# Value product of an attention layer turned round: v stationary on two column halves of the array, queries moving, probabilities divided on GpSimd

## The chip, the cores and the metric

One core of one Trainium2 chip. The metric is the device time of one launch in microseconds, median of several runs. In the profile PE is TensorE (PEld its weight loads), DVE is VectorE, ACT is ScalarE, POOL is GpSimd.

## The reference, cut to what matters

Input x has 64 batches of 256 tokens with 512 features, float32. Layer 0 is a graph attention, layer 1 a masked attention of 8 heads of 64 columns. Each is `x + layer(relu(layernorm(x)))`.

```
# layer 1, h = relu(layernorm(x)); adj is one 256x256 mask for all batches
q, k, v = split_heads(h @ Wq.T + bq), split_heads(h @ Wk.T + bk), split_heads(h @ Wv.T + bv)
scores = einsum('bhqd,bhkd->bhqk', q, k) / sqrt(64)
attn = softmax(where(adj == 0, -inf, scores))
out = einsum('bhqk,bhkd->bhqd', attn, v)         # <- the value product
return merge_heads(out) @ Wo.T + bo
```

## The kernel before

It works in 32 groups of two batches, that is four tiles of 128 tokens. Layer 0 of the next group is issued among layer 1 of this one. A unit of layer-1 attention is one tile and four heads, and unit n's values are issued behind unit n+1's scores:

```python
def values(t, hq, pr):                       # pr: numerators, queries on the partitions
    ...
    for i in range(2):
        # transpose two heads: keys onto the partitions
        nc.tensor.transpose(pp[:, r, kc, :], pr[:, 2 * i + r, kc * P : (kc + 1) * P], ident)
        ...copy pp to pT, DVE for i = 0, ACT for i = 1...
        nc.tensor.matmul(
            pav[:, h * DH : (h + 1) * DH],                  # [128 queries, 64]
            pT[:, r, kc, :],                                # stationary: 128x128 probabilities
            v[:, b * NC + kc, h * DH : (h + 1) * DH],       # moving: 64 columns
            start=(kc == 0), stop=(kc == NC - 1))

def finish(t):                               # once per tile
    nc.vector.reciprocal(rc, sm)
    nc.vector.tensor_mul(av, pav, rc)                       # normalise the output (broadcast cut)
    ...four transposes of av into pa, ACT copy to aT, output projection, residual, store...

for t in range(NT):
    for hq in range(2):
        pr = scores(t, hq)
        yield
        if pending is not None:
            values(*pending)
            if pending[1] == 1:
                finish(pending[0])
            yield
        pending = (t, hq, pr)
```

Layer 0 runs on the same engines in the same stretch:

```python
nc.vector.tensor_reduce(nmx, z, AX.X, ALU.max)                                  # 128x2
nc.vector.tensor_scalar(nmx, nmx, FLOOR, -1.0, op0=ALU.max, op1=ALU.mult)       # "the negation"
...exponentials on ACT, transposes pp, copy pT, then the layer-0 product po...
```

## Time and profile before

| | before |
|---|---|
| time, us (median; range) | 3982.18 (3979.65 to 3984.23) |
| mean granted clock | 0.998 |
| one group, us | 123.2: projections 55.1, attention 68.1 |

The page, the chain of waits and the timeline of one group are shown in the prediction. One more view of the kernel before cuts the attention stretch of that group (1963.60 to 2031.70) into pieces. The columns are start:end, length, then busy us of PE, PEld, DVE, ACT and POOL (with their instructions), the granted clock (PEclk), the DMA share and GB/s:

```profile
core 0: us, PE busy (x) PEld busy (x) DVE busy (x) ACT busy (x) POOL busy (x), PEclk, DMA share, GB/s
1963.60:1978.60 15.00, 14.56 (x86) 9.98 (x86) 13.99 (x55) 9.04 (x32) 0.00 (x0) 1.00 0.01 2
1978.60:1993.60 15.00, 14.82 (x68) 8.74 (x68) 9.28 (x27) 4.04 (x14) 0.00 (x0) 1.00 0.05 17
1993.60:2008.60 15.00, 14.79 (x91) 10.20 (x90) 12.05 (x40) 6.28 (x20) 4.57 (x4) 1.00 0.05 19
2008.60:2031.70 23.10, 20.84 (x127) 14.85 (x125) 9.06 (x21) 10.31 (x29) 2.88 (x2) 1.00 0.09 28
```

(The page counts records: the 2048 value matmuls of the program stand there as 4096, two each.) DVE, with 13.99 of 15 us, is the busiest engine of the opening after PE itself (14.56). One row of that group's timeline is for later: the first transposes of numerators, 4.57 us into the stretch.

```profile
1968.17 1.91 PE L322 MATMUL pp<-ident,pr 128*128 128x128 f32 x8
```

### The profile page before, as it was taken

Reading aid. Unit: us, or ns where it says so; the run is one execution under the profiler, and the core shown is the slowest. Engines: PE = TensorE matmul, PEld = TensorE weight load, DVE = VectorE, ACT = ScalarE, POOL = GpSimd, SP = SyncE. Lnnn points to the kernel's source line nnn. Section 1 sums busy time; section 2 is a strip of 40 time slices with the busy share of each in tenths; the row PEclk is TensorE's granted clock in tenths of the full one; section 3 lists DMA queues with packets and bytes.
Section 4 is the critical chain, followed back from the end, with each engine's and each line's share of the span. In section 5 each row is a group of like instructions: output and inputs, shape, how many; then the busy total and the mean of one; then the engine's idle time right before and its main releaser. Section 6 shows DMA issues by size and latency. Waiting matters only on the chain.

```text
span 3978.6 us, 41676 instructions
## 1 busy us (share of the span) xinstructions
PE 3853.1 (97%) x15744; PEld 2182.8 (55%) x15744; DVE 1732.9 (44%) x5186; ACT 1109.1 (28%) x3201; POOL 247.8 (6%) x206
## 2 busy tenths in 40 slices
PE   7999999999999999999999999999999999999999
PEld 3555555555555555555555555555555555555555
DVE  3444344443345433454334543344443444433442
ACT  1322223222233222332223322233222232222332
POOL 1000000000000000000000000000000000000000
PEclk9999999999999999999999999999999999999999
DMA  2000000000000000000000000000000000000000
GB/s 98 22 9 16 19 22 22 9 16 19 22 22 14 13 17 22 22 22 6 19 19 22 22 6 19 19 22 22 9 16 19 22 22 9 16 19 22 11 11 11
DMA packets 39144, 76.33 MB, mean 19 GB/s; under 512 B 3297, under 2 KB 3297, under 8 KB 38945
## 3 DMA queue, kind: packets, MB, share of 16 engines
q1 hardware_dynamic: 38480, 72.36, 5.0%
q8 instruction: 124, 2.03, 0.2%
q0 software_dynamic: 464, 1.32, 0.1%
q14 instruction: 76, 0.61, 0.1%
HBM read 40.11 MB, written 33.55 MB: 19 GB/s over the span
## 4 chain that ended last, share of the span: by engine, by line
PE 87%; DVE 9%; ACT 3%; issue 1%; DMA 0%; POOL 0%; POOLq 0%; DVEq 0%; ACTq 0%
PE pav L333 12%; PE po L150 12%; PE pq L157 11%; PE pw L150 11%; PE pv L150 11%; PE pk L157 11%; PE psc L281 5%; PE pp L322 5%; PE po L223 4%; ACT hT L143 2%; PE pa L354 2%; DVE s L292 2%; PE pt L142 2%; DVE av L346 2%; DVE x L230 1%; DVE junk L174 1%
## 5 line engine op out<-in xcount | busy, mean ns | idle before, releaser
L333 PEld LDWEIGHTS pav<-v,pT 128*128 128x128 f32 x4096 | 498.8, 191 | 136.5 <-issue 45.9
L308 ACT ACTIVATE pr<-s,nmx 128x256 f32<-128x256 f32 x1024 | 507.0, 497 | 180.1 <-DVE nmx L304 157.9
L333 PE MATMUL pav<-v,pT 128*128 128x64 f32 x4096 | 525.0, 276 | 6.9 <-DVE pT L329 4.8
L150 PE MATMUL po<-wo_sb,aT 128*128 128x512 f32 x1024 | 474.2, 606 | 3.2 <-ACT aT L356 0.7
L157 PE MATMUL pq<-hT,wq_sb 128*128 128x512 f32 x1024 | 463.6, 595 | 7.9 <-ACT hT L143 7.9
L157 PE MATMUL pk<-hT,wk_sb 128*128 128x512 f32 x1024 | 460.3, 592 | 0.0
L150 PE MATMUL pw<-w_sb,hT 128*128 128x512 f32 x1024 | 460.1, 592 | 0.0
L150 PE MATMUL pv<-wv_sb,hT 128*128 128x512 f32 x1024 | 444.7, 592 | 0.0
L252 DVE TENSOR_SCALAR kT<-pk,bk_c 128x512 f32<-128x512 f32 x128 | 96.1, 751 | 776.0 <-PE pk L157 776.0
L281 PE MATMUL psc<-kT,qT 64*128 64x256 f32 x2048 | 399.0, 413 | 8.4 <-DVE mx L292 6.4
L292 DVE CUSTOM_DVE_ANT_0 s<-psc,mbias 128x256 f32<-128x256 f32 x1024 | 384.3, 417 | 11.1 <-PE psc L281 6.8
L171 ACT COPY wh<-pw 128x512 f32<-128x512 f32 x128 | 74.9, 585 | 1100.2 <-PE pw L150 1100.2
L157 PEld LDWEIGHTS pk<-hT,wk_sb 128*128 128x128 f32 x1024 | 194.6, 190 | 244.9 <-issue 244.9
L150 PEld LDWEIGHTS pv<-wv_sb,hT 128*128 128x128 f32 x1024 | 194.6, 190 | 244.9 <-issue 244.9
L150 PEld LDWEIGHTS pw<-w_sb,hT 128*128 128x128 f32 x1024 | 194.7, 190 | 244.5 <-issue 244.5
L157 PEld LDWEIGHTS pq<-hT,wq_sb 128*128 128x128 f32 x1024 | 191.9, 190 | 245.2 <-issue 229.6
L322 PE MATMUL pp<-ident,pr 128*128 128x128 f32 x2048 | 311.6, 277 | 5.0
L327 ACT COPY pT<-pp 128x512 f32<-128x512 f32 x256 | 149.1, 582 | 581.1 <-PE pp L322 578.2
L150 PEld LDWEIGHTS po<-wo_sb,aT 128*128 128x128 f32 x1024 | 184.4, 190 | 217.3 <-issue 184.1
L322 PEld LDWEIGHTS pp<-ident,pr 128*128 128x128 f32 x2048 | 234.3, 145 | 83.6 <-issue 44.1
L281 PEld LDWEIGHTS psc<-kT,qT 64*128 64x128 f32 x2048 | 220.9, 185 | 100.1 <-issue 56.8
L174 DVE SCALAR_TENSOR_TENSOR junk<-wh,a_dst_b 128x512 f32<-128x512 f32 x128 | 88.5, 691 | 421.4 <-ACT wh L171 421.4
(57 smaller groups left out, 3103.3 us busy)
## 6 DMA issues: line engine op xcount, KB each, us to landing
x<-in_x_dram SPq DMA_DIRECT2D x64, 512.0 KB, 4.4
out_dram<-x SPq DMA_DIRECT2D x128, 256.0 KB, 2.0
w_sb<-in_L_gnn_W_dram SPq DMA_DIRECT2D x1, 1024.0 KB, 13.3
wq_sb<-in_L_gnn_Wq_dram SPq DMA_DIRECT2D x1, 1024.0 KB, 15.9
wk_sb<-in_L_gnn_Wk_dram SPq DMA_DIRECT2D x1, 1024.0 KB, 18.1
wv_sb<-in_L_gnn_Wv_dram SPq DMA_DIRECT2D x1, 1024.0 KB, 20.1
wo_sb<-in_L_gnn_Wo_dram SPq DMA_DIRECT2D x1, 1024.0 KB, 16.1
a_src_b<-in_L_gnn_a_src_dram POOLq DMA_DIRECT2D x1, 256.0 KB, 6.8
```

Source lines behind the costliest of these rows:

```text
L142: nc.tensor.transpose(pt[:, c, :], xn[:, c * P : (c + 1) * P], ident)
L150: nc.tensor.matmul(dst, hT[:, c, t * P : (t + 1) * P], w_t[:, c, :], start=(c == 0), stop=(c == DC - 1))
L157: nc.tensor.matmul(dst, w_t[:, c, e * P : (e + 1) * P], hT[:, c, :], start=(c == 0), stop=(c == DC - 1))
L174: nc.vector.scalar_tensor_tensor(junk, wh[:, t, :], 1.0, a, op0=ALU.mult, op1=ALU.mult, accum_out=dst[:, t : t + 1])
L223: nc.tensor.matmul(po, pT[:, mc, c * P : (c + 1) * P], wh[:, b * NC + mc, :], start=(mc == 0), stop=(mc == NC - 1),)
L252: nc.vector.tensor_scalar_add(kT[:, e, :], pk, bk_c[:, e : e + 1])
L281: nc.tensor.matmul(psc[r][:, i, :], qT[rows, e, t * P : (t + 1) * P], kT[rows, e, b * N : (b + 1) * N], start=True, stop=True,)
L292: nc.vector.tensor_tensor_reduce(out=s[:, j, :], in0=psc[r][:, i, :], in1=mbias[:, c, :], scale=1.0, scalar=FLOOR, op0=ALU.add, op1=ALU.ma ...
L308: nc.scalar.activation(pr[:, j, :], s[:, j, :], AF.Exp, bias=nmx[:, j : j + 1], accum_out=sm[:, h : h + 1])
L322: nc.tensor.transpose(pp[:, r, kc, :], pr[:, 2 * i + r, kc * P : (kc + 1) * P], ident)
L327: nc.scalar.copy(pT, pp)
L333: nc.tensor.matmul(pav[:, h * DH : (h + 1) * DH], pT[:, r, kc, :], v[:, b * NC + kc, h * DH : (h + 1) * DH], start=(kc == 0), stop=(kc == ...
```

## The change

Its intent: with v stationary (128 keys by 64 columns, two heads side by side on the two column halves) and 256 queries moving, half as many matmuls are issued (2048 records for 4096 before), and the result comes out with the features on the partitions, as the output projection wants it. So the transposes back go. But the sums now lie along the moving side, so the numerators are divided before the product here: that is given to GpSimd, which was nearly idle (6% busy). A unit becomes both tiles of a batch and four heads.

```diff
-    ps_tr = ctx.enter_context(tc.tile_pool(name="ps_tr", bufs=3, space=PSUM))
+    ps_tr = ctx.enter_context(tc.tile_pool(name="ps_tr", bufs=2, space=PSUM))
     ps_sc = ...
+    ps_av = ctx.enter_context(tc.tile_pool(name="ps_av", bufs=1, space=PSUM))
 # scores: now a loop over the two tiles c of a batch; behind the exponentials of each
+                rc = small.tile([P, HQ], F32, tag="rc1", name=f"rc1_{nm}")
+                nc.vector.reciprocal(rc, sm)
+                nc.gpsimd.tensor_tensor(
+                    pr, pr,
+                    rc.rearrange("p (h o) -> p h o", o=1).to_broadcast([P, HQ, N]),
+                    op=ALU.mult,
+                )
 # values: transposes per head over both tiles, then
-                            pav[:, h * DH : (h + 1) * DH],
-                            pT[:, r, kc, :],
+                            pav[r * DH : (r + 1) * DH, i, :],
                             v[:, b * NC + kc, h * DH : (h + 1) * DH],
+                            pTs[2 * i + r][:, kc, :],
+            nc.vector.tensor_copy(aT[:, hq * 2 : hq * 2 + 2, b * N : (b + 1) * N], pav)
 # finish
-            ...reciprocal, tensor_mul av, four transposes pa, ACT copy aT...
-        for t in range(NT):
+        for b in range(GB):
             for hq in range(2):
-                pr = scores(t, hq)
+                prs = yield from scores(b, hq)
                 ...values of the unit before...
```

More of the change, by code (lines that the diff above doesn't have):

```diff
@@ L261, in layer1 @@
         HQ = 4
-        state = {}
-        def scores(t, hq):
-            b, c = divmod(t, NC)
-            if hq == 0:
-                state[t] = (
-                    small.tile([P, HEADS], F32, tag="mx1", name=f"mx1_{g}_{t}"),
-                    small.tile([P, HEADS], F32, tag="sm1", name=f"sm1_{g}_{t}"),
-                )
-            mx, sm = state[t]
-            psc = [
-                ps_sc.tile([P, 2, N], F32, tag="sc", name=f"psc_{g}_{t}_{hq}_{r}") for r in range(2)
-            ]
-            for i in range(2):
-                for r in range(2):
-                    e = hq * 2 + i
-                    rows = slice(r * DH, (r + 1) * DH)
-                    nc.tensor.matmul(
-                        psc[r][:, i, :],
-                        qT[rows, e, t * P : (t + 1) * P],
-                        kT[rows, e, b * N : (b + 1) * N],
-                        start=True,
-                        stop=True,
-                    )
-            s = work.tile([P, HQ, N], F32, tag="s", name=f"s_{g}_{t}_{hq}", bufs=2)
-            for j in range(HQ):
-                i, r = divmod(j, 2)
-                h = hq * HQ + j
-                nc.vector.tensor_tensor_reduce(
-                    out=s[:, j, :],
-                    in0=psc[r][:, i, :],
-                    in1=mbias[:, c, :],
-                    scale=1.0,
-                    scalar=FLOOR,
-                    op0=ALU.add,
-                    op1=ALU.max,
-                    accum_out=mx[:, h : h + 1],
-                )
-            hs = slice(hq * HQ, (hq + 1) * HQ)
-            nmx = small.tile([P, HQ], F32, tag="nmx1", name=f"nmx1_{g}_{t}_{hq}")
-            nc.vector.tensor_scalar_mul(nmx, mx[:, hs], -1.0)
-            pr = work.tile([P, HQ, N], F32, tag="pr1", name=f"pr1_{g}_{t}_{hq}")
-            for j in range(HQ):
-                h = hq * HQ + j
-                nc.scalar.activation(
-                    pr[:, j, :], s[:, j, :], AF.Exp, bias=nmx[:, j : j + 1], accum_out=sm[:, h : h + 1]
-                )
-            return pr
@@ L313, in values, with scores @@
-        def values(t, hq, pr):
-            b = t // NC
-            if hq == 0:
-                state[t] += (ps_mm.tile([P, D], F32, tag="mm", name=f"pav_{g}_{t}"),)
-            pav = state[t][2]
-            for i in range(2):
-                pp = ps_tr.tile([P, 2, NC, P], F32, tag="tr", name=f"pp1_{g}_{t}_{hq}_{i}")
-                for r in range(2):
-                    for kc in range(NC):
+        aT = big.tile([P, DC, TOK], F32, tag="aT", name=f"aT_{g}", bufs=1)
+        def scores(b, hq):
+            prs = []
+            for c in range(NC):
+                t = b * NC + c
+                nm = f"{g}_{t}_{hq}"
+                psc = [
+                    ps_sc.tile([P, 2, N], F32, tag="sc", name=f"psc_{nm}_{r}") for r in range(2)
+                ]
+                for i in range(2):
+                    for r in range(2):
+                        e = hq * 2 + i
+                        rows = slice(r * DH, (r + 1) * DH)
+                        nc.tensor.matmul(
+                            psc[r][:, i, :],
+                            qT[rows, e, t * P : (t + 1) * P],
+                            kT[rows, e, b * N : (b + 1) * N],
+                            start=True,
+                            stop=True,
+                        )
+                s = work.tile([P, HQ, N], F32, tag="s", name=f"s_{nm}", bufs=2)
+                mx = small.tile([P, HQ], F32, tag="mx1", name=f"mx1_{nm}")
+                for j in range(HQ):
+                    i, r = divmod(j, 2)
+                    nc.vector.tensor_tensor_reduce(
+                        out=s[:, j, :],
+                        in0=psc[r][:, i, :],
+                        in1=mbias[:, c, :],
+                        scale=1.0,
+                        scalar=FLOOR,
+                        op0=ALU.add,
+                        op1=ALU.max,
+                        accum_out=mx[:, j : j + 1],
+                    )
+                nmx = small.tile([P, HQ], F32, tag="nmx1", name=f"nmx1_{nm}")
+                nc.vector.tensor_scalar_mul(nmx, mx, -1.0)
+                pr = work.tile([P, HQ, N], F32, tag="pr1", name=f"pr1_{nm}", bufs=4)
+                sm = small.tile([P, HQ], F32, tag="sm1", name=f"sm1_{nm}")
+                for j in range(HQ):
+                    nc.scalar.activation(
+                        pr[:, j, :], s[:, j, :], AF.Exp, bias=nmx[:, j : j + 1], accum_out=sm[:, j : j + 1]
+                    )
+                rc = small.tile([P, HQ], F32, tag="rc1", name=f"rc1_{nm}")
+                nc.vector.reciprocal(rc, sm)
+                nc.gpsimd.tensor_tensor(
+                    pr,
+                    pr,
+                    rc.rearrange("p (h o) -> p h o", o=1).to_broadcast([P, HQ, N]),
+                    op=ALU.mult,
+                )
+                prs.append(pr)
+                yield
+            return prs
@@ L322, in values @@
+        def values(b, hq, prs):
+            nm = f"{g}_{b}_{hq}"
+            pTs = []
+            for j in range(HQ):
+                pp = ps_tr.tile([P, NC, N], F32, tag="tr", name=f"pp1_{nm}_{j}")
+                for kc in range(NC):
+                    for c in range(NC):
                         nc.tensor.transpose(
-                            pp[:, r, kc, :], pr[:, 2 * i + r, kc * P : (kc + 1) * P], ident
+                            pp[:, kc, c * P : (c + 1) * P], prs[c][:, j, kc * P : (kc + 1) * P], ident
@@ L324, in values @@
                         )
-                pT = work.tile([P, 2, NC, P], F32, tag="pT1", name=f"pT1_{g}_{t}_{hq}_{i}")
-                if i:
+                pT = work.tile([P, NC, N], F32, tag="pT1", name=f"pT1_{nm}_{j}", bufs=5)
+                if j % 2:
                     nc.scalar.copy(pT, pp)
@@ L329, in values @@
                     nc.vector.tensor_copy(pT, pp)
-                for r in range(2):
-                    h = hq * HQ + 2 * i + r
-                    for kc in range(NC):
+                pTs.append(pT)
+                if j == 1:
+                    yield
+            pav = ps_av.tile([P, 2, N], F32, tag="av", name=f"pav_{nm}")
+            for i in range(2):
+                for kc in range(NC):
+                    for r in range(2):
+                        h = hq * HQ + 2 * i + r
                         nc.tensor.matmul(
-                            pav[:, h * DH : (h + 1) * DH],
-                            pT[:, r, kc, :],
+                            pav[r * DH : (r + 1) * DH, i, :],
                             v[:, b * NC + kc, h * DH : (h + 1) * DH],
+                            pTs[2 * i + r][:, kc, :],
                             start=(kc == 0),
@@ L339, in values @@
                         )
+            nc.vector.tensor_copy(aT[:, hq * 2 : hq * 2 + 2, b * N : (b + 1) * N], pav)
+            yield
         def finish(t):
-            _, sm, pav = state.pop(t)
-            rc = small.tile([P, HEADS], F32, tag="rc1", name=f"rc1_{g}_{t}")
-            nc.vector.reciprocal(rc, sm)
-            av = work.tile([P, HEADS, DH], F32, tag="av", name=f"av_{g}_{t}", bufs=2)
-            nc.vector.tensor_mul(
-                av,
-                pav.rearrange("p (h d) -> p h d", h=HEADS),
-                rc.rearrange("p (h o) -> p h o", o=1).to_broadcast([P, HEADS, DH]),
-            )
-            avf = av.rearrange("p h d -> p (h d)")
-            pa = ps_tr.tile([P, DC, P], F32, tag="tr", name=f"pa_{g}_{t}")
-            for c in range(DC):
-                nc.tensor.transpose(pa[:, c, :], avf[:, c * P : (c + 1) * P], ident)
-            aT = work.tile([P, DC, P], F32, tag="aT", name=f"aT_{g}_{t}", bufs=2)
-            nc.scalar.copy(aT, pa)
             po = ps_mm.tile([P, D], F32, tag="mm", name=f"po1_{g}_{t}")
-            project_rows(po, aT, wo_sb, 0)
+            project_rows(po, aT, wo_sb, t)
             nc.vector.tensor_add(xt[:, t, :], po, xt[:, t, :])
@@ L363, in layer1 @@
         pending = None
-        for t in range(NT):
+        for b in range(GB):
             for hq in range(2):
-                pr = scores(t, hq)
-                yield
+                prs = yield from scores(b, hq)
                 if pending is not None:
-                    values(*pending)
+                    yield from values(*pending)
                     if pending[1] == 1:
-                        finish(pending[0])
-                    yield
-                pending = (t, hq, pr)
-        values(*pending)
-        finish(pending[0])
-        yield
+                        for c in range(NC):
+                            finish(pending[0] * NC + c)
+                            yield
+                pending = (b, hq, prs)
+        yield from values(*pending)
+        for c in range(NC):
+            finish(pending[0] * NC + c)
+            yield
     def run(gen):
```

## The prediction

> **What bounds the kernel now**
>
> I read the page's busy shares first, then the chain that ended last, then the costliest groups, then the timeline of one group (two batches), to see where TensorE (PE) is full and where it waits.
>
> ```profile
> PE 3853.1 (97%) x15744; PEld 2182.8 (55%) x15744; DVE 1732.9 (44%) x5186; ACT 1109.1 (28%) x3201; POOL 247.8 (6%) x206
> ...
> PE 87%; DVE 9%; ACT 3%; issue 1%; DMA 0%; POOL 0%; POOLq 0%; DVEq 0%; ACTq 0%
> PE pav L333 12%; PE po L150 12%; PE pq L157 11%; PE pw L150 11%; PE pv L150 11%; PE pk L157 11%; PE psc L281 5%; PE pp L322 5%; PE po L223 4%; ACT hT L143 2%; PE pa L354 2%; DVE s L292 2%; PE pt L142 2%; DVE av L346 2%; DVE x L230 1%; DVE junk L174 1%
> ...
> L333 PE MATMUL pav<-v,pT 128*128 128x64 f32 x4096 | 525.0, 276 | 6.9 <-DVE pT L329 4.8
> ```
>
> PE carries 87% of the chain. The value product (pav) is 12% of it, the chain's largest line. DMA is nowhere. The steps DVE av and PE pa, 2% each, are the detour that normalises the output and transposes it back.
>
> ```profile
> 1963.59 0.73 PEld L281 LDWEIGHTS psc<-kT,qT 64*128 64x128 f32 x8 [0.76 <-issue]
> 1963.60 1.13 PE L281 MATMUL psc<-kT,qT 64*128 64x256 f32 x8
> ...
> 1964.66 0.43 PE L184 MATMUL per<-ident,ed 128*128 128x128 f32 x2
> ```
> ```profile
> 2008.65 2.00 PE L333 MATMUL pav<-v,pT 128*128 128x64 f32 x16
> 2010.58 0.70 PE L281 MATMUL psc<-kT,qT 64*128 64x256 f32 x4
> 2011.43 0.66 PE L354 MATMUL pa<-ident,av 128*128 128x128 f32 x4 [0.15 <-DVE av L346]
> ...
> 2031.70 3.70 PE L157 MATMUL pq<-hT,wq_sb 128*128 128x512 f32 x8 [0.23 <-ACT hT L143]
> ```
>
> Columns: start, length, engine, line, what.[...] Sixteen pav records take 1.93 us (2008.65 to 2010.58), 0.12 each, although only 64 columns move[...]. The score product on two row halves moves 256 columns, yet eight records pass in 1.06 us: its halves overlap. A group lasts 123.2 us (1908.46 to 2031.70, the pq starts of two groups): projections until 1963.6 (55.1 us, back to back on PE), then attention until 2031.7 (68.1 us), where PE waits often. The change lies in the second stretch alone.
>
> ```profile
> 2125.64 1.27 POOL L239 TENSOR_TENSOR x<-x,bo_b 128x512 f32<-128x512 f32 x1 [4.50 <-DVE xn L137]
> ```
> ```profile
> 2125.47 0.20 DVE L344 RECIPROCAL rc<-sm 128x8 f32<-128x8 f32 x1
> 2125.59 0.13 DVE L128 BATCH_NORM_AGGREGATE mv<-st 128x2 f32<-128x6 f32 x1
> 2125.75 1.18 DVE L130 TENSOR_SCALAR ve<-mv 128x4 f32<-128x4 f32 x1
> ```
>
> These rows matter most. ve, four columns wide, takes 0.17 us elsewhere. Here it starts while GpSimd runs and ends at 2126.93, as GpSimd ends (2126.91). Half of the ve and 32 of the xn are stretched this way[...]. Reciprocals and PSUM copies that fell in such windows kept their length.
>
> [...]
>
> **The change, part by part**
>
> *Value product.* 2048 instead of 4096 records (32 groups x 4 half-batches x 8 matmuls x 2). At the pace of psc: 2048 x 0.107 = 219 us, against 12% of 3979 = 477. Gain 258 us. Without overlap of the halves it would be 437 and the gain 40.
>
> *Return transpose gone.* Removes av (128 x 0.69 = 88 us, on the chain) and pa (2%, about 80 us). ACT loses 75 us of aT copies, off the chain. The new DVE copy of pav costs DVE as much as av did, but other PE work mostly lies beside it. Gain up to 168 us, so 426 in all, if no wait takes their place: 3980 - 426 = 3555.
>
> *Division before the product.* 256 GpSimd operations of 128x1024[...]. But each stands between the exponentials and the transposes, and the transposes of one head now need both tiles of a batch. Per pair of tiles one multiplication can follow the other only when the second tile's exponentials are done. Reciprocals double in number (256 x 0.156 - 128 x 0.20 = +14 us on DVE)[...].
>
> *PSUM.* ps_tr falls from 3 to 2 buffers: the third transpose of a set waits for the first one's copy.
>
> *Walk through one attention stretch.* I took the instruction order of the changed program on each engine and the durations above (s 0.35, exp four in 2.05, copy 0.6, stt 0.75, st 0.6, zmax and reduce 0.6 each), time zero being 1963.6:
> - Opening. DVE reaches recip(tile 0) at 6.15 as before. GpSimd runs 6.4 to 8.8. DVE's next tensor-scalar, nmx of layer 0, waits for that (before: about 6.5), and ACT's next exponentials with it: tile 1's run 10.0 to 12.1, GpSimd 12.6 to 15.0, and again a nmx of layer 0 waits inside. PE gets its first full set of transposes at 15.0 (before: 4.6) and the copy for the layer-0 product at 16.1. PE is nearly idle for ten microseconds that used to hold about 8 us of work.
> - Middle. Layer-0 products, values of batch 0 half 0: done at 28.3. Half 1: xn and ve fall under the multiplication of tile 3, aT is copied at about 39.5, PE idles about 2.8 us, output projections end at 43.8, all scores at 44.7. Before, the same work stood at 42.8 (from the end of po1 at 2027.1 back over 18.7 us of work and 2 us of waits).
> - End. The last scores' chain is PE, DVE 1.4, ACT twice 2.05[...]: values of half 0 wait on ACT's copy behind the exponentials (idle about 5 us), half 1 waits for GpSimd at 53.5, projections end at 63.4, and the transposes of the next group take 4.6 as before: 68.0.
> - I left out the drain from matmul to reader (0.2 us: the copy of a set of four transposes starts 0.64 after they do, not 0.44). Some nine exposed hops: +2 us.
>
> Result 70 us against 68.1: +1.9 x 32 = +60 us. The 13 us gained per group on PE are used up as waits.
>
> **The rivals**
>
> 1. *PE work counts, waits are covered*: 3555 to 3700. For it: 97% PE busy and large slack elsewhere. Against: PE busy hides waits (its ends are modelled), and in attention PE already waits for DVE and ACT.
> 2. *Waits replace the work* (the walk): 3950 to 4120. For it: ve and xn under GpSimd; the strict order exponentials, reciprocal, GpSimd, transposes.
> 3. *Halves do not overlap*: +218 us of PE work, partly inside waits: 4100 to 4200. Against: psc overlaps, and the order alternates the halves.
> 4. *No blocking of the tiny nmx*, only of wide operations: the opening shrinks by 4 to 5 us a group, 3850 to 3900. The trace shows it for a 128x4, so I think this less likely.
>
> **Range and chances**
>
> 4040 us. The walk's error is about 3 us a group either way, 100 us: 3880 to 4170. 2% limits are 3902 and 4061. Faster 0.17 (rivals 1 and 4), within 0.42, slower 0.41.
>
> **What would show it**
>
> - pav at about 0.107 a record; if 0.2, rival 3.
> - [...]
> - nmx rows of 1 us and more on DVE in the opening; if all stay at 0.16, rival 4.
> - PE waiting for POOL in the list of waits, and POOL on the chain with several per cent; if POOL is absent there, rival 1 holds.
> - The attention stretch near 70 us and projections still 55.

## More of the kernel before

"Granted clock" is the share of TensorE's full clock that the records show.

## The result, and the profile after

| | before | after |
|---|---|---|
| time, us (median; range) | 3982.18 (3979.65 to 3984.23) | 4093.48 (4092.57 to 4095.11) |
| ratio | | 1.0281 [1.0266, 1.0295] |
| mean granted clock | 0.998 | 0.943 |

The change makes the kernel slower by 2.8%. A ratio is the mean time of one kernel's fast runs over that of the other's in the same rounds, with a 95% interval, so it is not quite the ratio of the medians.

The page of the kernel after: the busy shares, the chain by engine, and two rows of the costliest groups (busy us, mean ns of one | idle time before, and what ended it).

```profile
PE 3826.2 (93%) x13184; PEld 1928.6 (47%) x13184; DVE 1899.2 (46%) x5314; ACT 1035.1 (25%) x3073; POOL 722.4 (18%) x462
...
PE 77%; DVE 13%; ACT 7%; POOL 2%; issue 1%; DMA 0%; ACTq 0%; DVEq 0%; POOLq 0%
...
L310 POOL TENSOR_TENSOR pr<-pr,rc 128x1024 f32<-128x1024 f32 x256 | 484.9, 1896 | 2791.7 <-DVE rc L309 2410.0
...
L345 PE MATMUL pav<-pT,v 128*64 128x256 f32 x2048 | 334.3, 414 | 7.6 <-DVE pT L336 3.1
```

PE has 2560 fewer matmuls, yet its busy time fell by 27 us only. In place of PE's 87% of the chain there are 77%; DVE and ACT went up from 9 and 3 to 13 and 7. POOL stands on it with 2% only. The same pieces of an attention stretch as above, for a group of the kernel after:

```profile
core 0: us, PE busy (x) PEld busy (x) DVE busy (x) ACT busy (x) POOL busy (x), PEclk, DMA share, GB/s
2018.58:2033.58 15.00, 12.42 (x43) 6.95 (x42) 14.27 (x47) 6.89 (x26) 3.79 (x2) 0.70 0.00 0
2033.58:2048.58 15.00, 15.00 (x58) 7.79 (x57) 10.68 (x32) 5.12 (x18) 3.79 (x2) 0.84 0.00 0
2048.58:2063.58 15.00, 11.65 (x58) 6.24 (x57) 13.63 (x35) 5.05 (x18) 7.85 (x6) 1.00 0.01 2
2063.58:2092.74 29.16, 25.84 (x132) 15.30 (x131) 12.65 (x34) 10.14 (x27) 7.07 (x5) 0.94 0.14 47
```

This is the view to learn from. PE "busy" in the second piece is 15.00 of 15, but its clock is 0.84, and in the first piece it issues 43 matmuls where it issued 86, at 0.70. The timeline of that opening shows why (start, length, engine, line, what, and in brackets the idle time before it with what ended it):

```profile
2018.58 1.13 PE L279 MATMUL psc<-kT,qT 64*128 64x256 f32 x8
...
2025.02 1.89 POOL L310 TENSOR_TENSOR pr<-pr,rc 128x1024 f32<-128x1024 f32 x1 [61.47 <-DVE rc L309]
...
2025.09 1.85 DVE L197 TENSOR_SCALAR nmx<-nmx 128x2 f32<-128x2 f32 x1
...
2025.23 2.07 PE L279 MATMUL psc<-kT,qT 64*128 64x256 f32 x4 [2.04 <-DVE mx L290]
...
2034.05 5.68 PE L224 MATMUL po<-wh,pT 128*128 128x512 f32 x8
...
2042.87 3.70 PE L224 MATMUL po<-wh,pT 128*128 128x512 f32 x8
```

PE idles 2.04 us for DVE's row maxima: its next record is a score product, whose buffer (there are three, `ps_sc`) DVE must first have read. This happens in every group. In the list of waits (who waited for whom: us in total, times, longest) the row stands so before and after:

```profile
PE psc L281 <- DVE mx L292: 6.4, 31, 0.2
PE psc L279 <- DVE mx L290: 69.8, 62, 2.0
```

In the kernel before, PE's transposes came from 4.57 us on, just where that hole begins now. The layer-0 product, PE's first long piece of work, starts at 2034.05, 15.5 us in, and its first eight records take 5.68 us; eight of the same records at full clock take 3.70. The clock records of this group show half the clock from 2024.58 for 13.65 us.

I then took, from each trace, means over its 31 full groups. Times are counted from the first score matmul of a group; "half clock" adds up all stretches of granted clock 0.5 in the whole run.

| mean us | before | after |
|---|---|---|
| projections | 55.13 | 55.13 |
| attention stretch | 68.05 | 71.75 |
| first layer-0 product | 9.94 | 15.45 |
| last score matmul | 47.29 | 47.37 |
| last output projection | 63.03 | 66.01 |
| half clock, whole run | 18 | 469 |

71.75 - 68.05 = 3.70 us a group, and 31 x 3.70 = 115 us: the whole loss of 111 us lies in the attention stretches.

### The profile page after: what moved, and what is told of

The parts are those of the page before. It is cut to its first block, busy times and chain, and to the rows that moved or that the text cites. A ratio compares the mean times of both kernels' runs of the same rounds, so it can differ in the third digit from the quotient of the medians.

```text
span 4092.3 us, 37025 instructions
## 1 busy us (share of the span) xinstructions
PE 3826.2 (93%) x13184; PEld 1928.6 (47%) x13184; DVE 1899.2 (46%) x5314; ACT 1035.1 (25%) x3073; POOL 722.4 (18%) x462
## 4 chain that ended last, share of the span: by engine, by line
PE 77%; DVE 13%; ACT 7%; POOL 2%; issue 1%; DMA 0%; ACTq 0%; DVEq 0%; POOLq 0%
PE pq L158 11%; PE pw L151 11%; PE pv L151 11%; PE pk L158 11%; PE po L151 9%; PE po L224 7%; PE pav L345 5%; PE psc L279 5%; ACT pr L305 5%; PE pp L329 4%; DVE s L290 4%; DVE xn L138 3%; PE pt L143 2%; PE pp L215 1%; POOL pr L310 1%; DVE nmx L197 1%
## 5 line engine op out<-in xcount | busy, mean ns | idle before, releaser
L310 POOL TENSOR_TENSOR pr<-pr,rc 128x1024 f32<-128x1024 f32 x256 | 484.9, 1896 | 2791.7 <-DVE rc L309 2410.0
L279 PE MATMUL psc<-kT,qT 64*128 64x256 f32 x2048 | 508.0, 450 | 70.1 <-DVE mx L290 69.8
L151 PE MATMUL po<-wo_sb,aT 128*128 128x512 f32 x1024 | 476.0, 603 | 36.7 <-DVE aT L352 36.7
L279 PEld LDWEIGHTS psc<-kT,qT 64*128 64x128 f32 x2048 | 301.2, 208 | 227.9 <-DVE mx L290 104.0
L345 PE MATMUL pav<-pT,v 128*64 128x256 f32 x2048 | 334.3, 414 | 7.6 <-DVE pT L336 3.1
L224 PE MATMUL po<-wh,pT 128*128 128x512 f32 x512 | 289.4, 717 | 0.0
```

The lines of the kernel that those rows point to most:

```text
L151: nc.tensor.matmul(dst, hT[:, c, t * P : (t + 1) * P], w_t[:, c, :], start=(c == 0), stop=(c == DC - 1))
L224: nc.tensor.matmul(po, pT[:, mc, c * P : (c + 1) * P], wh[:, b * NC + mc, :], start=(mc == 0), stop=(mc == NC - 1),)
L279: nc.tensor.matmul(psc[r][:, i, :], qT[rows, e, t * P : (t + 1) * P], kT[rows, e, b * N : (b + 1) * N], start=True, stop=True,)
L310: nc.gpsimd.tensor_tensor(pr, pr, rc.rearrange("p (h o) -> p h o", o=1).to_broadcast([P, HQ, N]), op=ALU.mult,)
L345: nc.tensor.matmul(pav[r * DH : (r + 1) * DH, i, :], v[:, b * NC + kc, h * DH : (h + 1) * DH], pTs[2 * i + r][:, kc, :], start=(kc == 0), ...
```

## The experiments

Twelve kernels ran, each timed in three rounds against the kernel before, whose medians lay between 3981 and 3984 us. Ratios are to it. Attention and "first product" are the group means defined above.

| run | us | ratio [95%] | clock | attention | first product |
|---|---|---|---|---|---|
| after | 4093.48 | 1.0281 [1.0266, 1.0295] | 0.943 | 71.75 | 15.45 |
| e1_no_division | 4046.09 | 1.0152 [1.0136, 1.0167] | 0.942 | 70.11 | 14.88 |
| e2_division_dve | 4125.55 | 1.0358 [1.0341, 1.0375] | 0.939 | 72.86 | 16.66 |
| e3_negate_on_act | 4060.83 | 1.0195 [1.0179, 1.0210] | 0.947 | 70.75 | 14.25 |
| e6_warm | 4215.85 | 1.0584 [1.0568, 1.0599] | 0.986 | 75.53 | 16.26 |
| f1_fine_no_division | 3711.42 | 0.9322 [0.9308, 0.9336] | 0.998 | 59.62 | 9.88 |
| f2_fine_division_pool | 4050.07 | 1.0172 [1.0157, 1.0187] | 0.927 | 70.29 | 14.99 |
| f3_three_buffers | 4125.40 | 1.0363 [1.0346, 1.0381] | 0.939 | 72.66 | 15.68 |
| f4_old_product_two_tiles | 4175.34 | 1.0487 [1.0472, 1.0503] | 0.955 | 74.36 | 15.41 |
| g1_late_v | 3959.38 | 0.9944 [0.9929, 0.9959] | 0.948 | 77.91 | 25.26 |
| g2_fine_pool_late_v | 3885.95 | 0.9757 [0.9743, 0.9772] | 0.978 | 75.30 | 21.65 |
| g3_before_late_v | 3915.68 | 0.9833 [0.9818, 0.9847] | 0.997 | 76.25 | 21.05 |
| g4_fine_pool_late_v_negate | 3891.47 | 0.9772 [0.9756, 0.9789] | 0.975 | 75.64 | 21.74 |

In the four g runs projections of 10.3 us a group moved into the attention stretch, so that column is not to be compared with the others there. e1 and f1 give wrong results (no division); all others are correct.

### First set: is it the division?

My first theory, the prediction's, was that the multiplication on GpSimd and its block of DVE cost the gain. Rivals: it is the waiting for GpSimd alone, or only the block.

**e1_no_division**: the changed kernel without the multiplication.

```diff
-                nc.gpsimd.tensor_tensor(pr, pr, ...rc broadcast..., op=ALU.mult)
```

> The changed kernel without the multiplication on GpSimd (reciprocals still computed; the result is wrong on purpose). Theory: the turned-round product is a gain and the division on GpSimd takes it back, by delaying the transposes and by holding VectorE's tensor-scalars. Then 3600 to 3720 us, the attention stretch 57 to 60 us, granted clock above 0.98. Rival: the product itself[...] costs the time; then 3950 or more.

Measured 4046 us: a miss. Leaving the whole division out wins 47 us of the 111 lost, let alone the 426 that the prediction gave to the turned product. 256 operations of 1.9 us are gone and the opening looks much the same. So in these units the division on its own is not what eats the gain. The time lies in the rival's range; f1 and f3 below test that rival.

**e2_division_dve**: the same division as four tensor-scalars on DVE.

```diff
-                nc.gpsimd.tensor_tensor(pr, pr, ...rc broadcast..., op=ALU.mult)
+                for j in range(HQ):
+                    nc.vector.tensor_scalar_mul(pr[:, j, :], pr[:, j, :], rc[:, j : j + 1])
```

> The division on VectorE, one tensor-scalar of 128x256 for each head, result right. Theory: no lock and a shorter step (about 1.2 us against 1.9), so 3680 to 3800 us, faster than before; VectorE busy rises by about 300 us but stays below 60%. Rival: any division ahead of the transposes costs what GpSimd's did, as it is the length of the chain that counts: 3980 to 4090.

Measured 4126 us, slower than on GpSimd: a miss again, and above the rival's range too. The operations are short (0.348 us mean, 1024 of them, which overlap and keep DVE busy for 292 us in all, 1.14 us for the four of a tile), and DVE's negation no longer waits (0.159 us mean, against 1.769 in the change). But DVE is the busiest engine of the opening after PE, so a likely reason is that these operations lengthen its queue; that was not tested.

**e3_negate_on_act**: the tiny negation, which waits for GpSimd, moved to ACT.

```diff
-            nc.vector.tensor_scalar(nmx, nmx, FLOOR, -1.0, op0=ALU.max, op1=ALU.mult)
+            nc.scalar.mul(nmx, nmx, -1.0)
```

> Only the negation of layer 0's maxima (a tensor-scalar of 128x2 that takes 1.85 us behind GpSimd) goes to ScalarE; the division stays on GpSimd. Result right, as each row has an edge. If the lock of VectorE in the opening is what costs, two times 1.7 us a group vanish, and some throttled clock with them: 3900 to 3990 us. If it is GpSimd's own duration in the chain: 4060 to 4095.

Measured 4061 us, in the range for GpSimd's own duration: the block is real, but to move the negation wins only 4093 - 4061 = 33 us, about 1 us a group. It is a minor part. The edit moves the block rather than ends it: 62 of DVE's clamps of layer 0's sums (`sm`) now begin under GpSimd and take 0.42 us (median) instead of 0.16.

**e6_warm**: sixteen idle matmuls of 128x256 a group in the hole, to keep the clock up without useful work.

```diff
+                if b == 0 and hq == 0:
+                    dummy = ps_av.tile([P, 2, N], F32, tag="av", name=f"dummy_{nm}")
+                    for d in range(8):
+                        nc.tensor.matmul(dummy[:, d % 2, :], ident, s[:, HQ - 1, :], start=True, stop=True)
```

> The changed kernel with sixteen idle matmuls of 128x256 a group in the opening's gap (into the bank of the value product, never read; result right). Theory: the halved clock (0.943 on average) costs on its own, as it lasts into the layer-0 product: clock above 0.98 and 3990 to 4050 us. Rival: the clock is halved only where TensorE has nothing to do: 4080 to 4110 us.

Both theories missed. The clock went up to 0.986 and half-clock time down to 121 us, but the time rose by 122 us. The dummies take PE time (1024 records, 237 us busy), and they read s, so they wait for DVE's last pass over the scores (43.5 us of idle PE before them ended with it) and hold up what stands behind them. Its total does not tell what the clock alone is worth (its single groups do, see below). It does tell that keeping PE busy with nothing is no cure.

### Second set: the product, the unit, the division, the buffers

Since e1 refuted the division as the only cause, I took the change apart: the unit of two tiles and the turned product are separate things.

**f1_fine_no_division** and **f2_fine_division_pool**: the units of the kernel before (one tile, four heads), with the product turned round (128 queries moving), no return transposes; f1 without the division, f2 with it on GpSimd. Both also take the reciprocals behind the exponentials and swap the two inner loops of the product, so that the column halves alternate; the cut below leaves this out.

```diff
 # f1, against the kernel before
-                            pav[:, h * DH : (h + 1) * DH],
-                            pT[:, r, kc, :],
+                            pav[r * DH : (r + 1) * DH, hq * 2 + i, :],
                             v[:, b * NC + kc, h * DH : (h + 1) * DH],
+                            pT[:, r, kc, :],
 # finish
-            ...reciprocal, tensor_mul av, four transposes pa...
-            nc.scalar.copy(aT, pa)
+            nc.vector.tensor_copy(aT, pav)
 # f2 adds
+            nc.gpsimd.tensor_tensor(pr, pr, ...rc broadcast..., op=ALU.mult)
```

> The kernel before in its own units (one tile, four heads) with only the product turned round: v stationary on two column halves, 128 queries moving; no return transpose, and no division (wrong on purpose). New theory: with the division taken away the changed kernel still took 4046 us, so it is the unit of two tiles that costs: TensorE must wait for the scores of two tiles at the start and end of each group, and its clock halves in the wait. Then in small units the product's gain shows: 3600 to 3750 us, clock above 0.98. Rival: the turned product is itself no gain[...]: 3900 or more.

> As the one above, with the division on GpSimd as in the change; result right. New theory: the division costs little, as without it the changed kernel gained 47 us: 3650 to 3850, faster than both kernels. Rival: in small units the division is exposed each time: 3900 to 4100.

f1 is a hit: 3711 us, 270 less than before, at a clock of 0.998. So the turned product is a real gain, even with 4096 records instead of 2048. f2, a miss in the rival's range, loses 339 us of it again: the division's cost is 339 us here and was 47 us in the two-tile units. Costs that don't add up like this suggest that both delays fall into one and the same wait. The PE rows at the start of one attention stretch of f1 show what the good case looks like:

```profile
1837.79 1.13 PE L281 MATMUL psc<-kT,qT 64*128 64x256 f32 x8
...
1842.37 1.92 PE L324 MATMUL pp<-ident,pr 128*128 128x128 f32 x8
...
1847.67 1.12 PE L223 MATMUL po<-wh,pT 128*128 128x512 f32 x2
```

Transposes 4.6 us in, layer-0 product 9.9 us in. The same place in e1, two-tile units without any division:

```profile
1998.17 1.13 PE L279 MATMUL psc<-kT,qT 64*128 64x256 f32 x8
...
2004.79 1.13 PE L279 MATMUL psc<-kT,qT 64*128 64x256 f32 x4 [2.02 <-DVE mx L290]
...
2009.16 1.11 PE L323 MATMUL pp<-ident,pr 128*128 128x128 f32 x4
2010.20 2.07 PE L279 MATMUL psc<-kT,qT 64*128 64x256 f32 x6
2012.21 5.79 PE L224 MATMUL po<-wh,pT 128*128 128x512 f32 x8
```

And in f2, small units with the division:

```profile
1999.45 1.13 PE L281 MATMUL psc<-kT,qT 64*128 64x256 f32 x8
...
2006.09 2.07 PE L281 MATMUL psc<-kT,qT 64*128 64x256 f32 x4 [2.04 <-DVE mx L292]
2008.09 1.97 PE L327 MATMUL pp<-ident,pr 128*128 128x128 f32 x8
```

Either one opens the same hole of 2 us. In e1 the transposes come 11.0 us in (a head's need the exponentials of both tiles), in f2 8.6 us in (they need GpSimd's result). In both, a further score product stands ahead of them in PE's order and is the one that waits, for DVE's row maxima; that the later transposes are why it stands there is argued from the rows, not tested. The hole is no wider when both are there (2.04 us), which fits that e1 bought so little.

**f3_three_buffers**: the changed kernel with the PSUM split of the kernel before.

```diff
-    ps_tr = ctx.enter_context(tc.tile_pool(name="ps_tr", bufs=2, space=PSUM))
+    ps_tr = ctx.enter_context(tc.tile_pool(name="ps_tr", bufs=3, space=PSUM))
-            pav = ps_av.tile([P, 2, N], F32, tag="av", name=f"pav_{nm}")
+            pav = ps_mm.tile([P, 2, N], F32, tag="mm", name=f"pav_{nm}")
```

> The changed kernel with three transpose buffers as before (the product takes a bank of the projections' pool). Theory of the two-tile unit: 4050 to 4100, within 1% of the change. Rival: the third buffer given up is what costs: 3990 or less.

4125 us, 25 above the range but within 1% of the change: the third transpose buffer isn't what was missed. The run was even 32 us slower; its pav now shares two buffers with the projections, which I did not look into further.

**f4_old_product_two_tiles**: the product, division and return transposes of the kernel before, in the two-tile units of the changed one.

```diff
-        for t in range(NT):
+        for b in range(GB):
             for hq in range(2):
-                pr = scores(t, hq)
-                ...values of (t, hq) before...
+                prs = [scores(b * NC + c, hq) for c in range(NC)]       # with a yield behind each
+                ...values of both tiles of the unit before, then finish of both...
```

> The kernel before with its own product, division at the end and return transpose, but in the units of the change: scores of two tiles, then values of two tiles, one step behind. Theory of the two-tile unit: slower than before by 3% and more, 4100 to 4350, with halved clock in the openings. Rival (unit harmless): 3960 to 4020.

A hit: 4175 us, 193 us slower than before, with the first product at 15.41 us and a clock of 0.955. No division before the product, no turned product, and the same late opening. The order of the two-tile unit is enough for it; in f4 each tile is transposed by itself, so it isn't that a head needs both tiles. Two reservations. The cut leaves out that f4 also makes the output and its division in two halves a tile: in the example group the first of these products comes 20.1 us in, behind the late opening, but part of the 193 us may be theirs. And layer 0's steps are issued at the yields of layer 1, so every two-tile kernel also places them differently: no run parts that from the unit itself.

### Third set: fill the hole with real work

The theory by now: the coarser unit, or the division, delays the first transposes; PE has nothing to do in a stretch that used to be full, its clock halves for some ten microseconds (13.65 in the group above), and the gain is gone. If so, giving PE ready work there must bring it back, with product and division untouched. The value projection of the second batch is such work: it isn't needed until that batch's values. One thing comes along, which the cut does not show: with the move a yield goes, so layer 0's steps fall one place later. The last of layer 0's four weight projections (pw) thus moves into the opening as well, and in all it is 10.3 us of work that moves, not the 6.9 us of the expectation below.

```diff
-        for t in range(NT):
-            ...project v of tile t...
+        for t in range(NC):
+            project_v(t)
 # behind the first two score tiles of the group
+                if b == 0 and hq == 0:
+                    project_v(NC + c)
```

**g1_late_v** is the changed kernel with this edit, **g2_fine_pool_late_v** is f2 with it, **g3_before_late_v** is the kernel before with it (the fair base), and **g4_fine_pool_late_v_negate** is g2 with e3's edit.

> The changed kernel, with the value projection of batch 1's two tiles moved from before the scores to behind the first two score tiles; product, division and units are untouched, and so is the amount of work. Theory (the loss is the gap at the opening of each attention stretch, in which TensorE has nothing to do and then runs at a lower granted clock): 6.9 us of ready work fill the gap, the mean granted clock goes from 0.943 to above 0.97, and the time to 3880 to 4000. Rival (the order of the projections doesn't matter, the loss is a chain of waits further on): 4060 or more, at a clock below 0.96.

> Units of one tile and four heads, product turned round, division on GpSimd, no return transpose (4050 us, clock 0.927), with the same late value projection. Correct results. Theory: the gap is filled, the clock is above 0.97, and the gain of the turned product appears: 3700 to 3880, faster than both kernels. Rival (the division costs its time wherever the projection stands): 3980 or more.

> The kernel before with the same late value projection: what the move is worth by itself. Theory: the opening before has hardly a gap and its clock is 0.998 already, so little: 3900 to 3985. If it gains as much as the other two, the move is a gain of its own and says nothing of the gap.

> As the run of small units with division and late projection, and layer 0's tiny negation on ScalarE, where GpSimd does not hold it up. Theory: what is left of the gap closes further: 3680 to 3860, no slower than that run. If the negation no longer stands on the path, the two agree within 0.5%.

g3, at 3916 us, shows that the move is a gain of its own: 66 us. On the changed kernel it is worth 4093 - 3959 = 134 us and on f2 4050 - 3886 = 164 us, so 69 and 99 us beyond the base: ready work (v's and pw's together) pays more where there is a hole. g1's time was as expected, its clock was not: 0.948 instead of over 0.97. The pieces of one attention stretch of g1 show where the hole went:

```profile
1946.25:1961.25 15.00, 15.00 (x55) 7.41 (x55) 7.70 (x30) 4.74 (x17) 2.59 (x2) 1.00 0.00 0
1961.25:1976.25 15.00, 12.42 (x46) 7.19 (x45) 14.78 (x46) 6.79 (x25) 4.98 (x3) 0.89 0.00 0
```

The first 15 us are full now, and the same hole, with DVE at 14.78 of 15, stands behind them: still 416 us of half clock in the run. The two-tile unit moves its wait along; it does not lose it. In g2 the opening is full, and what is left stands near the end of the stretch:

```profile
1908.57:1923.57 15.00, 14.62 (x55) 7.22 (x54) 7.70 (x30) 5.32 (x18) 2.60 (x2) 1.00 0.00 0
...
1953.57:1968.57 15.00, 10.33 (x69) 6.86 (x68) 10.29 (x27) 3.61 (x12) 7.63 (x6) 0.89 0.05 18
```

There PE waits twice, first for DVE's copy of transposes, then for GpSimd itself, as these rows of the same group's timeline say:

```profile
1958.65 1.97 PE L340 MATMUL pav<-pT,v 128*64 128x128 f32 x16 [2.40 <-DVE pT L336]
...
1966.54 0.76 PE L329 MATMUL pp<-ident,pr 128*128 128x128 f32 x5 [2.08 <-POOL pr L315]
```

g2 beats both kernels: 2.4% under the kernel before. Its expectation (3700 to 3880) was missed by 6 us, and most of what it wins is the move: against g3 it is 0.9757 / 0.9833 = 0.992. g4 agrees with g2 within 0.2%, as expected if the negation is off the path, though its range (3680 to 3860) was missed: with the opening filled, none of the 64 negations meets GpSimd any more (0.154 us median in g2), so nothing is left to win there.

## Why the prediction was right or wrong

The time, 4093 us, lay in the range and 53 above the middle. The class "slower" had 0.41, beside 0.42 for "within 2%". The range (3880 to 4170) was wider than the error of 100 us that was to justify it. The sign and the place were right; that the total came out so near is partly luck, as the steps show:

- **Value product.** Predicted 0.107 us a record, the pace of psc inside its run of eight. Measured: sixteen in 1.87 us (2079.36 to the next PE row, 2081.23, in the example group), 0.117. The halves overlap: in that run the records start in pairs 0.007 us apart, a pair about every 0.21 us. One by one at half of the 0.43 us that a record of 512 columns takes, 0.213 each (the 437 us of the prediction), they would have taken 3.4 us. Rival 3 is out. But that is an unbroken run. From each pav record to the next PE record, at full clock and with no step counted above 0.45 us, the mean over the trace is 0.151 us, against 0.118 before: an estimate of 2048 x 0.151 = 309 us instead of 219, and a gain of about 175 instead of 258. That the turned product gains at all is shown by f1: 270 us, against 426 predicted with no waits. Summed the same way, the product takes 485 us before and 299 in f1, and pa's steps come to 64: together 250 of the 270. The 88 us of av did not go, as a copy of pav of the same length took its place (128 of 0.68 us in f1).
- **GpSimd's multiplication.** Mis-sized: 1.90 us, in all 485. The walk lets it run 2.4 us (6.4 to 8.8); that was an estimate of mine, which no trace showed for this width.
- **Block of the tiny negation.** Right: 61 of 64 took over 1 us, mean below. To move it wins 33 us (e3), where rival 4 had put 4 to 5 us a group, about 150 us. The delay sits in a chain that waits for DVE anyhow. Which operations were held, the traces show one by one. In the kernel before, the 31 ve and 32 xn that began under a GpSimd operation took 1.18 and 1.50 us (medians) against 0.17 and 0.54 elsewhere; 31 copies of transposes from PSUM took 0.685 us and two reciprocals 0.20, as elsewhere. In g2 layer 0's leaky ReLU, which reads z from SBUF twice, took 1.33 us (median of 31) when it began under GpSimd against 0.68 elsewhere, while the score reduction, with one input from PSUM, stayed at 0.42 in both.

```profile
L138 DVE TENSOR_SCALAR xn<-x,mv,rstd 128x512 f32<-128x512 f32 x256 | 231.2, 943 | 33.3 <-POOL rstd L133 26.9 <-PE pt L143 6.4
...
L197 DVE TENSOR_SCALAR nmx<-nmx 128x2 f32<-128x2 f32 x64 | 113.2, 1769 | 0.0
...
L131 DVE TENSOR_SCALAR ve<-mv 128x4 f32<-128x4 f32 x64 | 14.8, 232 | 1.3 <-issue 0.2
```

- **Middle: "xn and ve fall under the multiplication of tile 3".** Half right. The rows above say that xn does (943 ns, with 92 of 256 over 1 us), but ve hardly: 232 ns, 3 of 64 over 1 us, against half of them in the kernel before.
- **Opening.** The layer-0 product was walked to about 16.1 us and stands at 15.45. But the reason given for it failed. The walk put the hole down to GpSimd and the blocked negation; e1 takes both away and the product still comes at 14.88. "The transposes of one head now need both tiles" stood in the prediction as a remark with no cost of its own; f4 shows that the order of the two-tile unit costs 193 us with the old product, even where each tile's transposes need that tile alone. The two delays lie beside each other, so the sum hid the error.
- **The clock.** Not in the walk at all, and the step that failed in size. It took all PE durations at full speed. In the run, the layer-0 product alone had about 130 steps at about 0.84 us where they take 0.44 at full clock, 130 x 0.40 = 52 us. Over all PE groups the same sum gives 165 us. It is rough: the score steps in it also contain waits for DVE, and steps from one line to another are left out.
- **Stretch.** Walked 70, measured 71.75: (71.75 - 70) x 31 = 54 us, which is the whole difference to the predicted time. All scores ended at 47.4 instead of 44.7 and the output projections at 66.0 instead of 63.4. The projections were 55.13, as said.
- **"POOL on the chain with several per cent".** It has 2%, and DVE and ACT took PE's share. In the list of waits PE waited for POOL once, 2.3 us; the walk had it wait in every group, near 53.5 us. By the prediction's own sign rival 1 (waits are covered) would then hold, and it does not: the sign was badly chosen. PE's largest waits are the 69.8 us for DVE's row maxima shown above, 56.0 us for ACT's copies of the numerators' transposes (32 times, at most 1.8 us, where the walk had about 5) and 36.7 us for DVE's aT copies. What GpSimd's multiplication costs in these units, e1 puts at 47 us in all. So the walk counted waits that did not come and left out the half clock; that these errors offset each other is likely, not shown.

How much of the loss is the idle hole, and how much the halved clock after it? e6 was to part them and failed, but the traces narrow it down. All groups of a run are the same code, yet the half-clock stretches fall differently in them. I left out each run's last group; medians of the attention stretch, with the number of groups:

| run | less half clock | more half clock | us per us of half clock |
|---|---|---|---|
| before | 68.10 at 0 (29) | 69.50 at 3.41 (1) | 0.41 |
| after | 71.49 at 13.65 (24) | 72.85 at 17.07 (6) | 0.40 |
| e1 | 68.23 at 10.24 (11) | 71.17 at 17.07 (16) | 0.43 |
| f2 | 66.23 at 10.24 (5) | 71.33 at 20.48 (24) | 0.50 |
| e6 | 74.06 at 0 (9) | 77.24 at 6.83 (10) | 0.47 |

The changed kernel has 14.3 us of half clock a group. At 0.4 us each this is an estimate of some 5.7 us, more than the 3.70 us lost: at full clock throughout it would be somewhat faster than the kernel before. In f2 the same sum puts most of the division's 339 us down to the clock: 71.33 - 20.48 x 0.50 = 61.1 us a stretch, against f1's 59.62. These estimates extrapolate beyond the groups measured, and they compare groups, not runs made for the purpose; the change at a full clock was never run. What stays open is also why the clock halves where it does.

## What to carry to other kernels

Before making a unit of work larger to save instructions, look at what the engine that is nearly always busy will do until the first large unit is ready: here two delays, each enough to empty the same few microseconds, turned a saving (270 us in f1) into a loss, most of it, by the estimate above, through the halved clock that followed a hole of 2 us. Test such causes singly and together, because costs that share one hole don't add, and taking away one of them shows almost nothing. Where a hole can't be avoided, move real work that is ready into it, and run the old kernel with the same move as the base.

## What the traces show of the clock, GpSimd and the column halves

- **Clock.** In the trace after, 51 of the 52 half-clock stretches lasted 3.41 (17 of them), 6.83 (2), 10.24 (12) or 13.65 us (20). In its example group the clock halved at 2024.58, within a step of 2.42 us between two matmul starts (2022.81 and 2025.23), the longest in that opening; in f4, with a longest step of 2.33 us, the mean clock of the first 15 us was 0.79. So no step above 2.5 us stood in these two openings. How long one has to be was not tested.
- **GpSimd.** The multiplication of 128x1024 with one operand broadcast took 1.90 us (mean of 256), the addition of 128x512 with none 1.27 us (median of 128 in the kernel after).
- **Column halves.** In an unbroken run the turned product keeps the old pace with half the records (2048 at 0.117 us for 4096 at 0.12), over the whole trace hardly (0.151 against 0.118). And a softmax's sums then lie along the moving side, so that the normalisation of the output could not stay as it was: dividing before the product cost 339 us in small units (f2 against f1), more than the 270 us won. Other places for the division were not tried.
